# A fused attention and expert layer on one core: the mixed rounds issued in program order, two stores moved

## The chip, the cores and the metric

The kernel runs on one core of one Trainium2 chip. The metric is the device time of one execution in microseconds; the median of three runs is compared. Engines are called PE (TensorE), DVE (VectorE), ACT (ScalarE), POOL (GpSimd) and SP (SyncE, which issues the DMAs here).

## The reference

The input `x` has 2 batches of 512 tokens with 512 channels, all in f32. It is normalized per token, and two branches are added to it.

```python
xn = _layernorm(x, axis=-1)
x = x + _L0_attn_ref(xn, qkv_w, out_w, gate_w, norm_w) + _L0_ffn_ref(xn, W_base, b_base, W_router, A, B)

# attention: 32 heads of 128, blocks of 32 tokens, a state kv of 128 x 128 per head
qkv = silu(xn @ qkv_w.T)                       # 3 x 32 x 128 outputs
scores = einsum('bhnd,bhmd->bhnm', cq, ck) * diag_decay
intra = einsum('bhnm,bhmd->bhnd', scores, cv)
inter = einsum('bhnd,bhde->bhne', cq * q_decay, kv)
kv_next = kv * block_decay + einsum('bhnd,bhne->bhde', ck * k_decay, cv)
attn = intra + inter, for all heads side by side
out = (sigmoid(xn @ gate_w.T) * norm_w * attn * rsqrt(mean(attn ** 2) + eps)) @ out_w.T

# expert branch: base_out = xn @ W_base.T + b_base, plus two of eight rank-16 experts for each token
```

## The kernel before

The three large projections (values, gate, queries and keys) are done with a two-level Strassen scheme. Sixteen sets of weights are worked through, `n = 0` to `15`; set 8 and later (`n >= VG`) hold queries and keys. Each set has seven outer products `q`, and each (set, outer product) is one *round* in the list `rounds`. A round has seven *inner products* `i`, each of two matmuls of 256 columns (L299 for values, L302 for gate, queries and keys). A slot `k` of the main loop holds one inner product, in the order of `SLOTS`, which mixes the tail of one round with the head of the next. A set takes 49 slots.

`encode` makes a round's operands on POOL two rounds ahead: `s` (L156, L168), then four `e` pieces (L175 to L181). `load_block` brings the weights as `raw` (L144). After each inner product, `after` takes the partial sum out of its PSUM bank: ACT copies `pa` to `pb` (L374) and `pb` to `pd` (L385), DVE adds (`put` L353, `taken` L368, and L394), and when a piece of a query or key is complete, ACT applies silu (L327).

When all pieces of one head and batch are there, `complete` makes an *item*; there are 64. `attend` is a generator whose steps do the item's attention:

- DVE transposes the keys in squares of 32 (`squares`, L488); SP stores them to DRAM (`k_kept`, L490) and loads two masks (L493, L494);
- SP loads them back as transposed keys `kt` in four DMAs (L499), and the values `v` (L501);
- PE multiplies keys and queries into `pc`, DVE applies the mask (`scores`, L508), POOL decays the queries (`qd`, L511), SP loads `gate` (L514);
- ACT scales `kt` to `kd` (L518);
- PE multiplies `kd` and `v` into `pu`, and DVE sums the `state` (L526, L528);
- PE makes `pa` from `scores`, `v`, `qd` and `state`; ACT squares it (`sq`, L542), POOL adds the squares up (`ssq`, L543), DVE applies the gate (`gT`, L545), and SP stores the result (`g_kept`, L546).

The matmuls of `attend` go through the helper `mm` (L89). The first two steps are put at fixed distances from completion by the table `later`; the other steps are drawn from `stages` at 24 steps in 49 slots, which is one item in 6.1 slots. A slot of the query and key sets thus mixes an inner product with some attention: these are the *mixed rounds*. They begin at the round `(VG, 1)`.

After the loop the remaining items are finished, together with the first part of the output projection, again a Strassen scheme: `load_gated` brings back the stored results (L641), `load_out_w` brings `wo` (L634) and scales it on ACT by the norm weights (L636), `operands` makes `gsum` on DVE (L647 to L650) and `wsum` on POOL (L654 to L657), `out_product` multiplies (L666). The first three of 16 pairs of heads (`EARLY = 3`) are multiplied while the last items are finished; the others follow in the part called `late`.

Buffers are rings: `scores`, `gate` and `mask` have three tiles, `kt`, `kd`, `state` and `gT` two, `e` three, `qk` and `v` five, and the PSUM tags `fr` and `sc` two banks each, `at` one. A tile is written again only after its last reader is through.

The order of instructions on each engine is not the order in the code: a scheduler takes the instructions from the code and places them by its own costs and priorities, and adds the semaphores. Each engine then works through its list in that order.

Of the kernel before, what the change touches and what calls it, by code (L numbers as in the profile page):

```python
# [60 lines left out]
def attn_moe_kernel(ctx: ExitStack, tc: tile.TileContext, x, qk_w, v_w, gate_w, out_w, norm_w,  # L61
# [17 lines left out]
    def bank(tag):  # L79
        return ps.tile([P, 512], F32, tag=tag, name=f"ps_{tag}", bufs=banks[tag])  # L80
# [392 lines left out]
    def complete(item):  # L473

        items.append(item)
        g = running[len(items) - 1] = attend(*item)
        ready[len(items) - 1] = now[0] + 4
        later[now[0] + 2].append(g)
        later[now[0] + 6].append(g)

    def attend(head, b):

        s_, u, f = head // 8, head // HG % 2, head % HG
        q, k = qk[head, b][:, 0], qk.pop((head, b))[:, 1]


        squares = work.tile([P, 4, TB - 1, 32], F32, tag="squares", name="squares", bufs=2)
        nc.vector.transpose(squares.rearrange("p c j d -> p j c d"), k[:, : (TB - 1) * P])  # L488
        kept = dram.tile([P, 4, TB - 1, 32], F32, tag="k_kept", name="k_kept", bufs=3)
        nc.sync.dma_start(kept, squares)  # L490
        mask = work.tile([P, 2, P], F32, tag="mask", name="mask", bufs=3)

        nc.sync.dma_start(mask[:, 0, :], decay[head][:, :P])  # L493
        nc.sync.dma_start(mask[:, 1, :], decay[head][P - 1, P : 2 * P].partition_broadcast(P))  # L494
        yield

        kt = work.tile([P, 4, TB - 1, 32], F32, tag="kt", name="kt", bufs=2)
        for c in range(4):
            nc.sync.dma_start(kt[32 * c : 32 * c + 32], kept[:, c].rearrange("(a i) j d -> i a j d", a=4))  # L499
        v = ring("v")  # L500
        nc.sync.dma_start(v, v_kept[s_][:, u, f, b, :])  # L501
        yield

        pc = bank("sc")
        for j in range(TB):
            mm(pc[:, j * P : (j + 1) * P], k[:, j * P : (j + 1) * P], q[:, j * P : (j + 1) * P], True, True)
        sc = ring("scores", [P, TB, P])
        nc.vector.tensor_tensor(sc, pc.rearrange("p (j n) -> p j n", j=TB),  # L508
                                mask[:, 0, :].unsqueeze(1).to_broadcast([P, TB, P]), ALU.mult)
        qd = work.tile([P, TB - 1, P], F32, tag="qd", name="qd", bufs=3)  # L510
        nc.gpsimd.tensor_tensor(qd, q[:, P:].rearrange("p (j n) -> p j n", j=TB - 1),  # L511
                                mask[:, 1, :].unsqueeze(1).to_broadcast([P, TB - 1, P]), ALU.mult)
        gate = ring("gate")
        nc.sync.dma_start(gate, gate_kept[s_][:, u, f, b, :])  # L514
        yield

        kd = work.tile([P, TB - 1, P], F32, tag="kd", name="kd", bufs=2)
        nc.scalar.activation(kd.rearrange("p j (a d) -> p a j d", a=4), kt, AF.Copy,  # L518
                             scale=mask[:, 0, P - 1 : P])
        yield  # L520

        pu = bank("sc")
        for j in range(TB - 1):
            mm(pu[:, j * P : (j + 1) * P], kd[:, j, :], v[:, j * P : (j + 1) * P], True, True)
        state = work.tile([P, TB - 1, D], F32, tag="state", name="state", bufs=2)
        nc.vector.tensor_copy(state[:, 0, :], pu[:, :P])  # L526
        for j in range(1, TB - 1):
            nc.vector.scalar_tensor_tensor(state[:, j, :], state[:, j - 1, :], BLOCK_DECAY[head],  # L528
                                           pu[:, j * P : (j + 1) * P], ALU.mult, ALU.add)
        yield  # L530
        pa = bank("at")
        for j in range(TB):
            o = pa[:, j * P : (j + 1) * P]
            mm(o, v[:, j * P : (j + 1) * P], sc[:, j, :], True, j == 0)
            if j:
                mm(o, state[:, j - 1, :], qd[:, j - 1, :], False, True)
        if b not in seen:
            seen.add(b)
            nc.scalar.activation(ssq[b], pa, AF.Square)
        else:  # L540
            sq = ring("sq")
            nc.scalar.activation(sq, pa, AF.Square)  # L542
            nc.gpsimd.tensor_tensor(ssq[b], ssq[b], sq, ALU.add)  # L543
        gT = ring("gT")
        nc.vector.scalar_tensor_tensor(gT, gate, 1.0, pa, ALU.add, ALU.mult)  # L545
        nc.sync.dma_start(g_kept[head // 2][:, :, head % 2, b, :], gT.rearrange("p (f s) -> p f s", f=2))  # L546
        yield

# [3 lines left out]
    def stages():  # L552


        for i in range(ITEMS + 2):
            if i < ITEMS:
                while i not in ready or ready[i] > now[0]:
                    yield None
                next(running[i])
            if 1 <= i <= ITEMS:  # L560
                next(running[i - 1])
            if i < ITEMS:
                yield True
            if 1 <= i <= ITEMS:
                next(running[i - 1])
                yield True
            if i >= 2:
                next(running[i - 2])
                yield True

    stage = stages()
# [1 line left out]

    SLOTS = ((0, 1), (0, 5), (0, 2), (1, 7), (0, 6), (0, 3), (1, 4))
    credit = 0.0
    for k in range(7 * len(rounds) + 7):
        now[0] = k
        r0, m = divmod(k, 7)
        if m == 0:
            if r0 == 2:  # L580
                route()
            if r0 == 5:
                transpose_experts()
            if r0 in range(8, 8 + 3 * NT, 3):
                experts((r0 - 8) // 3)
            if r0 + 2 < len(rounds):
                coming = encode(*rounds[r0 + 2])
            if r0 < len(rounds):
                n, q = rounds[r0]
                state_of[r0] = {}  # L590
                for _, to in ADDED[q]:
                    if to == "u3":
                        outer_sums[n, to] = outer_sums[n, "u2"]
                    elif isinstance(to, str):
                        if (n, q) == (1, 1):

                            t = [ring("qk", [P, 2, 512]) for _ in range(2)]
                            outer_sums[n, to] = [t[ij // 2][:, ij % 2] for ij in range(4)]
                        else:
                            t = aw2.tile([P, 4, 512], F32, tag="sum", name="sum", bufs=3)  # L600
                            outer_sums[n, to] = [t[:, ij] for ij in range(4)]
                if n + 1 < NSET:
                    for fo, ko in {5: ((0, 0),), 7: ((1, 0), (1, 1)), 3: ((0, 1),)}.get(q, ()):
                        if (n + 1, fo, ko) not in blocks:
                            load_block(n + 1, fo, ko)
        for g in later.pop(k, ()):
            next(g)
        if r0 + 2 < len(rounds):
            next(coming, None)
        back, i = SLOTS[m]  # L610
        r = r0 - back
        if 0 <= r < len(rounds):
            st = state_of[r]
            if i in (1, 5):
                st["pa" if i == 1 else "pc"] = bank("fr" if kind(rounds[r][0]) == 2 or i == 1 else "sc")
            inner_product(st[{1: "pa", 2: "pa", 5: "pc", 3: "pc", 6: "pb", 7: "pd", 4: "pd"}[i]], r, i, i in (1, 5))
            after(r, i)
        if items:
            credit = min(credit + 24 / 49, 1.5)
            if credit >= 1 and next(stage):  # L620
                credit -= 1
# [47 lines left out]
    EARLY = 3  # L669
    sums = [{}, {}]  # L670
    early = iter([(i, n) for i in range(EARLY) for n in FIRST])
    for k in sorted(later):
        for g in later[k]:
            next(g)
    now[0] += 4
    for i in range(EARLY):
        load_gated(0, i)
        load_out_w(i)
    load_out_w(EARLY)
    left = 0  # L680
    while True:
        s_ = next(stage, "end")
        if s_ == "end":
            break
        if s_:
            left += 1
            if left == 3:
                sums[0].update({1: bank("fr"), 6: bank("fr"), 5: seeded[0], 7: seeded[1]})
                for i in range(EARLY):
                    operands(0, i)  # L690
            if left >= 5:
                for e in [next(early, None)]:
                    if e:
                        out_product(0, *e, sums[0])
    for e in early:
        out_product(0, *e, sums[0])
    attention.close()
    late = ctx.enter_context(tc.tile_pool(name="late", bufs=1))

# [122 lines left out]
```

## Time and profile before

| | us |
|---|---|
| median of three runs (1211.67 to 1215.09) | 1213.78 |
| profiled execution, its own time | 1215.73 |
| profiled execution, span of the core | 1213.8 |

| engine | busy us | share of the span | instructions |
|---|---|---|---|
| PE | 1155.9 | 95% | 6024 |
| PEld (weight loads) | 996.8 | 82% | 6024 |
| DVE | 750.9 | 62% | 1350 |
| ACT | 431.8 | 36% | 764 |
| POOL | 737.8 | 61% | 798 |

The profile is of one execution. A matmul of the program shows as two records. "Busy" is the time with an instruction on the engine; a time in square brackets or after "idle before" is the engine's idle time ahead of an instruction, with what released it. `SPq` is SP's sequencer: its time is that of issuing a DMA, and its waits are for semaphores. A line number in the profile is that of the kernel before; a line such as L89 or L353 can serve many uses, so the tile names tell what is meant.

### The profile page before, as it was taken

The page shows a single profiled execution, that of the slowest core. Times are in us where ns is not written, and L with a number is a line of the kernel's source. Part 1 is how long each engine was busy: PE and PEld are TensorE (multiplying, and loading weights), DVE is VectorE, ACT ScalarE, POOL GpSimd, SP SyncE. Part 2 cuts the span into 40 slices and gives each one's busy share as a digit, 9 for nine tenths or more (in the row PEclk, how much of TensorE's full clock was granted, in tenths as well). Part 3 has the DMA queues.
Part 4 walks back from the last instruction along what each step waited for, and adds up shares of the span by engine and source line. Part 5 has one row for each costly group of instructions (what it writes and reads, how often), then busy time and mean ns, then how long its engine had stood idle before and what let it go on. Part 6 is the DMA issues. An engine that isn't in the chain of part 4 may idle for free.

```text
span 1213.8 us, 17996 instructions
## 1 busy us (share of the span) xinstructions
PE 1155.9 (95%) x6024; PEld 996.8 (82%) x6024; DVE 750.9 (62%) x1350; ACT 431.8 (36%) x764; POOL 737.8 (61%) x798
## 2 busy tenths in 40 slices
PE   6999999999999999999999998988989968999998
PEld 5588888888888889999888987877878857888887
DVE  7477676675666686767767665646746745436334
ACT  3244434434444444343434333333333323300000
POOL 5166977766776775775856746448375335645552
PEclk9999999999999999999999999999999998999999
DMA  6335565544444544656556463463555568823221
GB/s 237 126 109 179 165 199 191 170 143 156 154 135 154 168 124 144 200 179 184 164 151 198 143 188 122 140 203 119 163 183 140 172 180 280 312 105 122 87 88 52
DMA packets 188139, 195.03 MB, mean 161 GB/s; under 512 B 50064, under 2 KB 159632, under 8 KB 187792
## 3 DMA queue, kind: packets, MB, share of 16 engines
q1 hardware_dynamic: 188048, 193.89, 50.7%
q8 instruction: 48, 0.79, 0.3%
q14 instruction: 43, 0.35, 0.1%
HBM read 124.06 MB, written 69.76 MB: 160 GB/s over the span
## 4 chain that ended last, share of the span: by engine, by line
PE 73%; POOL 5%; DMA 4%; issue 4%; DVE 3%; SPq 2%; ACT 1%; DVEq 0%; POOLq 0%; ACTq 0%
PE ps_fr L302 16%; PE sd L302 14%; PE ps_at L89 6%; PE ps_sc L89 6%; PE sd L666 6%; PE ps_fr L666 5%; PE ps_sc L666 5%; PE sd L299 4%; PE ps_sc L302 4%; PE ps_fr L299 3%; PE ps_sc L299 3%; DMA k_kept<-squares 2%; PE ps_at L666 1%; DVE qk L353 1%; POOL s L156 1%
## 5 line engine op out<-in xcount | busy, mean ns | idle before, releaser
L543 POOL TENSOR_TENSOR ssq<-ssq,sq 128x512 f32<-128x512 f32 x62 | 79.1, 1276 | 175.8 <-ACT sq L542 168.8
L302 PE MATMUL sd<-xt,e 128*128 128x256 f32 x672 | 169.4, 381 | 0.0
L302 PEld LDWEIGHTS sd<-xt,e 128*128 128x128 f32 x672 | 125.4, 191 | 16.0 <-ACT sd L385 0.3
L327 ACT ACTIVATE qk<-qk 128x512 f32<-128x512 f32 x128 | 80.2, 630 | 137.1 <-DVE qk L353 136.8
L368 DVE TENSOR_TENSOR w<-sd,sum 128x512 f32<-128x512 f32 x110 | 74.3, 686 | 54.2 <-ACT sd L385 53.6
L175 POOL TENSOR_TENSOR e<-s 128x256 f32<-128x256 f32 x64 | 47.7, 745 | 84.4 <-PE sd L302 65.4
L89 PE MATMUL ps_at<-scores,v 128*128 128x128 f32 x512 | 90.3, 279 | 2.8 <-DVE gT L545 2.8
L542 ACT ACTIVATE sq<-ps_at 128x512 f32<-128x512 f32 x62 | 37.0, 597 | 148.3 <-PE ps_at L89 147.2
L374 ACT COPY sd<-ps_fr 128x512 f32<-128x512 f32 x112 | 64.3, 574 | 70.8 <-PE ps_fr L302 44.4
L302 PE MATMUL ps_fr<-xsum,s 128*128 128x256 f32 x288 | 77.8, 388 | 7.4 <-DVE qk L353 7.2
L385 ACT COPY sd<-sd 128x512 f32<-128x512 f32 x112 | 64.3, 574 | 57.5 <-PE sd L302 47.5
L89 PEld LDWEIGHTS ps_at<-scores,v 128*128 128x128 f32 x512 | 76.2, 195 | 5.6 <-issue 2.8
L156 POOL TENSOR_TENSOR s<-raw 128x1024 f32<-128x1024 f32 x32 | 75.8, 2370 | 8.0 <-PE sd L302 4.9
L89 PE MATMUL ps_at<-qd,state 128*128 128x128 f32 x384 | 76.0, 280 | 0.1
L89 PE MATMUL ps_sc<-v,kd 128*128 128x128 f32 x384 | 55.5, 281 | 19.4 <-ACT kd L518 19.2
L647 DVE TENSOR_TENSOR gsum<-gated 128x256 f32<-128x256 f32 x32 | 15.6, 486 | 94.3 <-PE ps_sc L666 91.0
L89 PEld LDWEIGHTS ps_sc<-v,kd 128*128 128x128 f32 x384 | 51.0, 191 | 27.2 <-ACT kd L518 24.6
L654 POOL TENSOR_TENSOR wsum<-wo 128x256 f32<-128x256 f32 x32 | 24.8, 774 | 78.6 <-PE sd L666 45.8
L89 PE MATMUL ps_sc<-qk 128*128 128x128 f32 x512 | 70.6, 283 | 0.5 <-DVE scores L508 0.4
L89 PEld LDWEIGHTS ps_sc<-qk 128*128 128x128 f32 x512 | 66.8, 198 | 2.9 <-DVE state L528 0.7
L302 PEld LDWEIGHTS ps_fr<-xsum,s 128*128 128x128 f32 x288 | 50.9, 190 | 22.2 <-ACT sd L374 7.2
L511 POOL TENSOR_TENSOR qd<-qk,mask 128x384 f32<-128x384 f32 x64 | 65.4, 1024 | 4.1 <-ACT qk L327 2.5
(249 smaller groups left out, 2912.1 us busy)
## 6 DMA issues: line engine op xcount, KB each, us to landing
v_kept<-v SPq DMA_DIRECT2D x64, 256.0 KB, 2.5
gate_kept<-v SPq DMA_DIRECT2D x64, 256.0 KB, 2.6
gate<-gate_kept SPq DMA_DIRECT2D x64, 256.0 KB, 3.2
raw<-in_qk_w SPq DMA_DIRECT2D x64, 256.0 KB, 4.5
v<-v_kept SPq DMA_DIRECT2D x64, 256.0 KB, 2.9
g_kept<-gT SPq DMA_DIRECT2D x64, 256.0 KB, 3.1
gated<-g_kept SPq DMA_DIRECT2D x32, 512.0 KB, 3.6
k_kept<-squares SPq DMA_DIRECT2D x64, 192.0 KB, 3.2
```

The source lines that it names most:

```text
L89: nc.tensor.matmul(o, lhsT, rhs, start=start, stop=stop)
L156: nc.gpsimd.tensor_tensor(t, a, b, op)
L175: nc.gpsimd.tensor_tensor(e[:, 0], a21, a22, ALU.add)
L299: nc.tensor.matmul(o.rearrange("p (g j d) -> p j g d", g=2, j=2)[:, u], x_[:, u * P : (u + 1) * P], a, start=first and u == 0, stop=True, ...
L302: nc.tensor.matmul(o[:, u * HB : (u + 1) * HB], a[:, u], x_, start=first and u == 0, stop=True, skip_group_check=True)
L327: nc.scalar.activation(v, v, AF.Silu)
L368: nc.vector.tensor_tensor(o, v, t, ALU.add)
L374: nc.scalar.copy(st["pb"], st["pa"])
L385: nc.scalar.copy(st["pd"], st["pb"])
L511: nc.gpsimd.tensor_tensor(qd, q[:, P:].rearrange("p (j n) -> p j n", j=TB - 1), mask[:, 1, :].unsqueeze(1).to_broadcast([P, TB - 1, P]), A ...
L543: nc.gpsimd.tensor_tensor(ssq[b], ssq[b], sq, ALU.add)
L666: nc.tensor.matmul(sums[n][:, i * HO : (i + 1) * HO], l[:, i * P : (i + 1) * P], r, start=p == 0 and i == 0, stop=p == NP - 1, skip_group_ ...
```

## The change

A context `tc.manual_schedule` over all five engines is entered at the round `(VG, 1)` and left after the first part of the output projection. Within it the scheduler doesn't reorder: each engine takes the instructions in the order of the code. Instructions after the context are still placed by the scheduler, and some of them are put between those inside it.

With it the order in the code is changed:

- The `k_kept` store and the masks get a step of their own, one slot after the transposition; the `g_kept` store gets a step two slots after `gT`.
- In a slot, `encode`'s step now comes after the inner product.
- In the end part, the loads of `load_gated` and `load_out_w`, which stood ahead of the loop over the remaining steps, are made in its third step; `operands` are made in steps 7 to 9 instead of all in step 3; from step 8 on two output products are issued in a step, where one was from step 5 on. The last item's remaining step of `later` is made in step 4.

```diff
 def complete(item):
-        later[now[0] + 2].append(g)
-        later[now[0] + 6].append(g)
+        for slots in (2, 3, 6):
+            later[now[0] + slots].append(g)
...
         nc.vector.transpose(squares.rearrange("p c j d -> p j c d"), k[:, : (TB - 1) * P])
+        yield
         kept = dram.tile([P, 4, TB - 1, 32], F32, tag="k_kept", name="k_kept", bufs=3)
         nc.sync.dma_start(kept, squares)
...
         nc.vector.scalar_tensor_tensor(gT, gate, 1.0, pa, ALU.add, ALU.mult)
+        yield
         nc.sync.dma_start(g_kept[head // 2][:, :, head % 2, b, :], gT.rearrange("p (f s) -> p f s", f=2))
...
                 next(running[i - 2])
+                later[now[0] + 2].append(running[i - 2])
                 yield True
...
+    in_order = ctx.enter_context(ExitStack())
     for k in range(7 * len(rounds) + 7):
...
+            if r0 < len(rounds) and rounds[r0] == (VG, 1):
+                in_order.enter_context(tc.manual_schedule(engines={getattr(mybir.EngineType, e) for e in (
+                    "PE", "Activation", "DVE", "Pool", "SP")}))
...
-        if r0 + 2 < len(rounds):
-            next(coming, None)
         back, i = SLOTS[m]
...
             after(r, i)
+        if r0 + 2 < len(rounds):
+            next(coming, None)
...
-    for k in sorted(later):
-        for g in later[k]:
-            next(g)
+    def pass_on():
+        for k in sorted(later):
+            for g in later.pop(k):
+                next(g)
+
+    last = later.pop(max(later))
+    pass_on()
     now[0] += 4
-    for i in range(EARLY):
-        load_gated(0, i)
-        load_out_w(i)
-    load_out_w(EARLY)
     left = 0
-    while True:
-        s_ = next(stage, "end")
-        if s_ == "end":
-            break
-        if s_:
-            left += 1
-            if left == 3:
-                sums[0].update({1: bank("fr"), 6: bank("fr"), 5: seeded[0], 7: seeded[1]})
-                for i in range(EARLY):
-                    operands(0, i)
-            if left >= 5:
-                for e in [next(early, None)]:
-                    if e:
-                        out_product(0, *e, sums[0])
+    for s_ in stage:
+        left += 1
+        if left == 4:
+            for g in last:
+                next(g)
+        if left == 3:
+            for i in range(EARLY):
+                load_gated(0, i)
+                load_out_w(i)
+            load_out_w(EARLY)
+            sums[0].update({1: bank("fr"), 6: bank("fr"), 5: seeded[0], 7: seeded[1]})
+        if 7 <= left < 7 + EARLY:
+            operands(0, left - 7)
+        if left >= 8:
+            for e in [next(early, None), next(early, None)]:
+                if e:
+                    out_product(0, *e, sums[0])
+        if left > 1:
+            pass_on()
+    pass_on()
     for e in early:
         out_product(0, *e, sums[0])
+    in_order.close()
     attention.close()
```

## The prediction, made before the changed kernel was run

> **What bounds the kernel now.** I read the page's parts 1 and 2 first (PE is busy for 95% of the span), then the busy times by stretch, then who waited for whom on PE and on SP's queue, and last the timelines around single gaps.
>
> Columns below: stretch in us, its length, busy us (instructions) of PE, PEld, DVE, ACT, POOL, granted clock, DMA share, GB/s.
> ```profile
> 430.00:700.00 270.00, 269.77 (x1632) 243.13 (x1631) 190.21 (x352) 115.25 (x204) 183.21 (x189) 1.00 0.56 164
> 700.00:965.00 265.00, 239.88 (x1417) 211.72 (x1415) 162.77 (x312) 95.81 (x170) 148.55 (x153) 0.98 0.53 158
> 965.00:1030.00 65.00, 49.12 (x298) 43.24 (x299) 33.77 (x66) 20.46 (x36) 31.04 (x32) 0.93 0.75 230
> ...
> 1030.00:1210.00 180.00, 180.00 (x832) 158.04 (x830) 74.94 (x154) 16.92 (x26) 86.41 (x112) 1.00 0.37 128
> ```
> TensorE sets the time, and it is starved only in the second half of the mixed rounds and at their end: 25.1 us idle in 700 to 965, 15.9 in 965 to 1030, nothing before or after. No other engine is full there (DVE 61%, POOL 56%). A finer measure is the distance from one matmul's start to the next, less its shape's median step (216 ns for 256 columns, 112 ns for 128). The excess sums to 3.7 us in 425 to 700, 36.8 in 700 to 950, 25.5 in 950 to 1035, and zero after. It also holds what runs at half clock. These 62 us are what can be won.
>
> PE's waits in 700 to 1030 (us in total, times, longest), then SP's in 700 to 1000:
> ```profile
> PE ps_sc L89 <- ACT kd L518: 19.2, 11, 2.5
> PE ps_fr L302 <- DVE qk L353: 7.2, 4, 2.3
> PE sd L302 <- DVE qk L353: 4.9, 3, 1.7
> ```
> ```profile
> SPq L499 <- DMA k_kept<-squares: 29.3, 18, 3.6
> SPq L499 <- ACT kd L518: 29.0, 12, 4.3
> SPq L490 <- DVE squares L488: 25.2, 7, 8.8
> SPq L546 <- DVE gT L545: 20.0, 6, 5.2
> ```
> Half of PE's waiting is for `kd`, which ACT makes from `kt`, which comes through SP. One case in the timelines of SP and PE:
> ```profile
> 708.78 0.49 SPq L494 DMA_DIRECT2D mask<-in_decay  x1
> 711.77 0.57 SPq L546 DMA_DIRECT2D g_kept<-gT  x1
> 712.82 2.18 SPq L499 DMA_DIRECT2D kt<-k_kept  x4
> ```
> ```profile
> 719.26 0.94 PE L89 MATMUL ps_sc<-v,kd 128*128 128x128 f32 x6 [2.48 <-ACT kd L518]
> ```
> SP is held from 709.3 to 711.8 at the store of `gT`; the load of `kt` stands behind it, `kd` starts at 718.6, and PE stops 2.5 us. The waits for `qk` come from POOL: an `ssq` addition stood early in POOL's queue, held 7.0 us for its square, with `s` (2.35 us) and `qd` behind it; DVE's write of `qk` waited for that `qd` (2.56 us at 742.0).
>
> **What the Trainium skill says.** "TensorE: Matmul & The Clock Gate", section "Architectural detail", says that ACT and DVE are strict FIFO and GpSimd FIFO per core, so an instruction that waits holds all behind it; the POOL case agrees. "Perfetto Trace Analysis", "DMA Instruction — HWDGE", puts the semaphore wait of a DMA into the issuing sequencer; the 2.5 us at L546 agree. Part 1 of the first page gives a half clock after an idle window of about 3.4 us. Here gaps of 2.3 to 2.5 us are already followed by it (clock 0.63 in 719.6 to 723.0); (1 - clock) x time gives 5.3 us for 700 to 965 and 4.6 for 965 to 1030.
>
> **The change, part by part.** No instruction is added or removed; order and places change.
>
> *Both stores later.* The `k_kept` store and its two mask loads move from slot +2 after an item's completion to +3, the `g_kept` store two slots behind `gT`. A slot is one inner product, 4 x 216 ns, plus its share of attention (28 records x 112 ns an item, one item in 6.1 slots): 1.37 us. Transpose (0.57) and `gT` (square 0.60, then 0.68) are then mostly done when SP comes, so of L490's 25.2 and L546's 20 us little stays. Half the items load `kt` one slot after the store, which takes 3.2 us to land: SP still waits some 1.8 us there. SP's issues of an item (store 0.55, masks 0.85, `kt` 1.75, `v` 0.43, gate 0.45, `g_kept` 0.55, weights 0.6) are 5.2 us of the 8.4 that PE gives an item; with waits about 7. What the delay costs: store to `kd` is at least seven slots, 9.6 us, against 3.2 + 1.75 + 2.0 (landing of `kt`) + 0.5 = 7.5; `kd` (0.61) has two slots more to its matmuls. Cover: 4.2 us.
>
> *Program order.* By the order in the code, PE waits for nothing nearer than two slots back: `kd` and ACT's copy of `pa` two, DVE's `put` results three. ACT (43% busy) and POOL (68%, operands made seven slots ahead) keep up. POOL's `ssq` now stands at its own `pa`, and `encode` after the matmul it waits for, so the 7 us hold goes. DVE is tightest: the two rounds after a (n, 7) hold 17 additions (0.61 us start to start) and 16.5 us with attention (2.7 an item), of 19.2. Walking them by hand, DVE lags PE by up to 3 us and the next `fr` bank is free 0.4 us late. I take 0.8 us a set: 6.4 in eight sets, bounds 0 and 20. The other excess I carry over from the dense stretch: 3.7 / 275 x 525 = 7.1. So 425 to 950 goes from 40.5 to 13.5: **27.0 us won**.
>
> *The end of the mixed rounds.* Here a new wait arises. At `left == 3` three `gated` loads, four `wo` loads and eight ACT scalings are emitted, ahead of `kd` of item 61. Before, the scheduler kept all `kd` ahead:
> ```profile
> 1004.99 0.61 ACT L518 ACTIVATE kd<-kt,mask 128x384 f32<-128x384 f32 x1
> 1006.93 1.33 ACT L636 ACTIVATE wo<-wo,nw 128x512 f32<-128x512 f32 x2 [1.33 <-DMA wo<-in_out_w]
> ...
> 1012.89 2.62 ACT L636 ACTIVATE wo<-wo,nw 128x512 f32<-128x512 f32 x4 [1.22 <-DMA wo<-in_out_w]
> ```
> Now ACT waits for seven 512 KB loads. From the issue of the first (1001.31) to the last scaling (1015.5) took 14.2 us. Count from the end of the last inner product: addition, silu and `kd` of item 60 end at 2.1 us; SP, held at `kt` of 62 by that `kd` (two `kt` buffers), issues `kt`, `v`, two stores, masks and gate and reaches `gated` at 6.7; scalings end at 20.9, `kd` of 61 at 21.5. PE does 1.6 us of products and idles from 3.6 to 21.5, **18 us**, plus 1.7 of half clock; then 1 us for `kd` of 62, some 3.5 for POOL's `wsum` (four of 0.75 behind an `ssq` and a `qd`), 1.6 before at `kd` of 60, rest 1.5. Sum 27, bounds 12 and 38, against 25.5 before: **1.5 us lost**. What SP, DVE and POOL hold behind this is long ready.
>
> *Sum.* 25.5 us off the profiled execution (1215.7; span 1213.8) gives 1190. The median of the runs is 2 us under that execution: **1188**.
>
> **Rivals.**
> - As worked, 1180 to 1197: 0.52.
> - The end is shorter (loads reach HBM sooner, or SP arrives early): 12 instead of 27 gives 1173, range 1168 to 1180: 0.17. Speaks for it: 230 GB/s in the stretch, while landings 1.28 us apart inside the burst make 410. Against: the order on ACT is fixed.
> - Strict order costs more on DVE, ACT or POOL, 1 to 3 us a set more: 1196 to 1210: 0.15. For it: DVE was 98% busy in 440 to 450. Against: nothing stalled there.
> - Slower: `kt` comes too late for `kd` in strict ACT order. 32 items have seven slots from store to `kd`; if SP is over 4.2 us late, PE stops each time, and ACT's copies behind `kd` stop too. From 1 us an item on, 32 us eat the gain; at 1.5 us it is 48, giving 1236. For it: SP's listed waits were as large in the dense stretch. Against: these waits came mostly from the stores now moved. 0.11, with an end of 38 us included.
> - It does little: PE's order hardly moves in the mixed rounds (pairs of one product put together, `pu` a place earlier), so if SP's waits only change names, 1213 +- 3.5: 0.05.
>
> **How the numbers follow.** 0.3% (3.6 us) is about what a measurement can tell from no change. Faster 0.52 + 0.17 + 0.15 = 0.84, same 0.05, slower 0.11. The range 1168 to 1208 holds the first three.
>
> **What would show it.** Right: PE 1.00 busy from 430 to some 950, waits of PE on `kd` there under 5 us, SP's waits at both stores nearly gone; then one PE gap of 14 to 20 us before `ps_sc<-v,kd`, released by ACT, with ACT's `wo` scalings waiting for DMA; the last inner product near 955 instead of 978. Wrong: repeated short PE gaps on DVE `qk` or ACT `kd` in each set, or no long gap at the end.

## The result, and the profile after

The changed kernel takes **1201.42 us** (median of four runs, 1197.69 to 1203.17), the kernel before 1213.32 (1211.67 to 1215.09). The ratio is 0.9898 [0.9868, 0.9927]: faster by 1.0%, where 1188 us, 2.1%, was forecast. The profiled execution took 1197.69 us, its span is 1195.9.

Busy times by stretch in the changed kernel; the columns are those shown for the kernel before:

```profile
430.00:700.00 270.00, 264.36 (x1624) 240.81 (x1623) 190.72 (x355) 112.81 (x200) 179.08 (x187) 1.00 0.62 180
700.00:965.00 265.00, 251.43 (x1566) 228.61 (x1564) 182.72 (x346) 105.98 (x188) 163.73 (x167) 1.00 0.62 179
965.00:1030.00 65.00, 46.13 (x244) 41.37 (x245) 29.70 (x52) 25.82 (x41) 29.77 (x35) 0.83 0.78 266
```

PE loses less in 700 to 965 (13.6 us idle where it was 25.1), but now 5.6 in 430 to 700, where it lost nothing, and more in the end (18.9 for 15.9). The fences of this part name the lines of the changed kernel (L327 to L374 are the same, `kd` is L519, the stores L491 and L548), those of an experiment the lines of its own kernel. The finer measure of the prediction, the excess of start-to-start distances over the shape's median:

| us | to 425 | 425 to 700 | 700 to 950 | 950 to 1035 | sum |
|---|---|---|---|---|---|
| before | 13.3 | 3.7 | 36.9 | 25.5 | 79.4 |
| forecast for after | 13.3 | 13.5 for 425 to 950 | | 27 | 53.8 |
| after | 14.1 | 8.0 | 9.4 | 29.9 | 61.4 |

The sum falls by 18.0 us, and the profiled executions differ by 18.0 (1215.73 to 1197.69): the table accounts for all of it. PE's waits in 400 to 1040 of the changed kernel (total, times, longest):

```profile
PE ps_sc L89 <- ACT kd L519: 22.0, 3, 20.2
PE ps_fr L302 <- ACT sd L374: 12.4, 12, 1.6
PE sd L674 <- POOL wsum L665: 3.5, 1, 3.5
PE ps_fr L302 <- DVE qk L353: 1.3, 2, 0.8
```

The waits for `kd` in the loop are gone (all three are after 955), those for `qk` nearly. In their place PE waits for ACT's copy of `pa` (L374): all twelve waits are before 950, and seven of them, of 0.9 to 1.6 us, come one in each set. At the end PE waits once for 20 us for `kd`. This long stop, on ACT and then on PE:

```profile
955.83 0.60 ACT L519 ACTIVATE kd<-kt,mask 128x384 f32<-128x384 f32 x1
959.08 0.60 ACT L543 ACTIVATE sq<-ps_at 128x512 f32<-128x512 f32 x1 [2.65 <-PE ps_at L89]
971.06 1.33 ACT L644 ACTIVATE wo<-wo,nw 128x512 f32<-128x512 f32 x2 [11.38 <-DMA wo<-in_out_w]
974.33 1.33 ACT L644 ACTIVATE wo<-wo,nw 128x512 f32<-128x512 f32 x2 [1.94 <-DMA wo<-in_out_w]
976.88 2.60 ACT L644 ACTIVATE wo<-wo,nw 128x512 f32<-128x512 f32 x4 [1.21 <-DMA wo<-in_out_w]
979.39 0.60 ACT L519 ACTIVATE kd<-kt,mask 128x384 f32<-128x384 f32 x1
```

```profile
958.82 1.06 PE L89 MATMUL ps_sc<-qk 128*128 128x128 f32 x8
980.04 1.65 PE L89 MATMUL ps_sc<-v,kd 128*128 128x128 f32 x6 [20.17 <-ACT kd L519]
...
990.72 1.22 PE L674 MATMUL sd<-wsum,gated 128*128 128x256 f32 x2 [3.47 <-POOL wsum L665]
```

ACT stands idle from 959.7 to 971.1, with `kd` of item 61 queued behind scalings whose weights are still on the way. The seven small stops have one form, once a set; this is one of them:

```profile
729.10 1.03 PE L302 MATMUL ps_fr<-xnT,raw 128*128 128x256 f32 x4
...
729.61 0.63 ACT L327 ACTIVATE qk<-qk 128x512 f32<-128x512 f32 x1 [2.72 <-DVE qk L353]
...
730.09 0.68 DVE L353 TENSOR_TENSOR qk<-sd,sum 128x512 f32<-128x512 f32 x1
730.80 0.63 ACT L327 ACTIVATE qk<-qk 128x512 f32<-128x512 f32 x1 [0.56 <-DVE qk L353]
731.34 0.58 ACT L543 ACTIVATE sq<-ps_at 128x512 f32<-128x512 f32 x1
731.82 0.59 ACT L374 COPY sd<-ps_fr 128x512 f32<-128x512 f32 x1
```

The first product of the round is complete at about 730.0, but its copy starts at 731.82: ahead of it ACT has a silu that waits for DVE's sum of the round before, then `sq`, which squares an attention result. PE, which needs the copy, stands 1.47 us, to 732.46.

SP's waits in 700 to 1000:

```profile
SPq L500 <- DMA k_kept<-squares: 50.5, 19, 4.3
SPq L491 <- DVE squares L488: 27.7, 9, 5.5
SPq L548 <- DVE gT L546: 14.8, 6, 8.9
```

SP waits more than before for the stored keys (50.5 us for 29.3), and as much at their store (27.7 for 25.2; L490 before, L491 now). PE does not stop for it: in the loop it no longer waits for `kd`.

### The profile page after: what moved, and what is told of

The parts are those of the page before. It is cut to its first block, busy times and chain, and to the rows that moved or that the text cites. A ratio compares the mean times of both kernels' runs of the same rounds, so it can differ in the third digit from the quotient of the medians.

```text
span 1195.9 us, 18068 instructions
## 1 busy us (share of the span) xinstructions
PE 1139.2 (95%) x6024; PEld 991.4 (83%) x6024; DVE 756.7 (63%) x1350; ACT 430.1 (36%) x764; POOL 735.4 (61%) x798
## 4 chain that ended last, share of the span: by engine, by line
PE 72%; DVE 6%; issue 4%; DMA 4%; ACT 2%; POOL 1%; SPq 1%; DVEq 0%; ACTq 0%; POOLq 0%
PE ps_fr L302 15%; PE sd L302 14%; PE ps_at L89 6%; PE ps_sc L89 6%; PE sd L674 6%; PE ps_sc L674 5%; PE ps_fr L674 5%; PE sd L299 5%; PE ps_sc L302 4%; PE ps_fr L299 3%; PE ps_sc L299 3%; DMA mask<-in_decay 2%; DVE qk L353 2%; DVE sum L353 1%; PE ps_at L674 1%
## 5 line engine op out<-in xcount | busy, mean ns | idle before, releaser
L327 ACT ACTIVATE qk<-qk 128x512 f32<-128x512 f32 x128 | 80.6, 630 | 245.3 <-DVE qk L353 245.3
L302 PE MATMUL sd<-xt,e 128*128 128x256 f32 x672 | 165.9, 379 | 0.0
L546 DVE SCALAR_TENSOR_TENSOR gT<-gate,ps_at 128x512 f32<-128x512 f32 x64 | 43.7, 684 | 78.9 <-ACT sq L543 74.7
L374 ACT COPY sd<-ps_fr 128x512 f32<-128x512 f32 x112 | 64.4, 575 | 48.3 <-PE ps_fr L302 23.5
L302 PE MATMUL ps_fr<-xsum,s 128*128 128x256 f32 x288 | 75.4, 384 | 1.1 <-ACT sd L374 0.9
L662 POOL TENSOR_TENSOR wsum<-wo 128x256 f32<-128x256 f32 x32 | 25.2, 788 | 78.5 <-PE sd L674 60.7
L175 POOL TENSOR_TENSOR e<-raw 128x256 f32<-128x256 f32 x48 | 35.9, 748 | 56.6 <-PE sd L302 30.4
L89 PE MATMUL ps_sc<-qk 128*128 128x128 f32 x512 | 67.5, 275 | 0.0
```

The source lines that it names most:

```text
L89: nc.tensor.matmul(o, lhsT, rhs, start=start, stop=stop)
L175: nc.gpsimd.tensor_tensor(e[:, 0], a21, a22, ALU.add)
L302: nc.tensor.matmul(o[:, u * HB : (u + 1) * HB], a[:, u], x_, start=first and u == 0, stop=True, skip_group_check=True)
L327: nc.scalar.activation(v, v, AF.Silu)
L374: nc.scalar.copy(st["pb"], st["pa"])
```

## The experiments

In one table first; ratios are to the kernel before in the same comparison. There were four comparisons (e0 to e3; e4 to e8; e9 to e12; e13 to e16), and the kernel before took 1212.8 to 1214.7 us in them, so a difference in us between two comparisons can be off by 2. "Loop" means that the context is closed ahead of the end part, and the end part is emitted as in the kernel before. The stores are moved unless it says otherwise.

| kernel | us | ratio [95%] |
|---|---|---|
| e0: the changed kernel again | 1200.49 | 0.9897 [0.988, 0.9913] |
| e1: `wo` scaled later | 1187.35 | 0.9789 [0.9769, 0.981] |
| e2: loop, all five engines | 1188.30 | 0.9797 [0.9783, 0.9812] |
| e3: stores only | 1213.34 | 0.9996 [0.9986, 1.0007] |
| e4: stores not moved | 1201.68 | 0.9897 [0.9879, 0.9914] |
| e5: silu later | 1193.44 | 0.9824 [0.9805, 0.9842] |
| e7: loop, silu later | 1177.37 | 0.9693 [0.9671, 0.9714] |
| e8: loop, POOL alone | 1200.50 | 0.9896 [0.9879, 0.9913] |
| e9: loop, all but POOL | 1188.59 | 0.9803 [0.9777, 0.9829] |
| e10: loop, POOL and SP | 1210.49 | 0.9981 [0.997, 0.9993] |
| e11: loop, POOL and PE | 1196.28 | 0.9878 [0.9855, 0.9902] |
| e12: loop, POOL, ACT, DVE | 1177.21 | 0.9705 [0.9689, 0.9722] |
| e13: loop, ACT, DVE | 1177.93 | 0.9707 [0.9683, 0.9731] |
| e14: loop, ACT alone | 1180.40 | 0.9728 [0.9714, 0.9743] |
| e15: loop, DVE alone | 1172.29 | 0.9659 [0.9642, 0.9675] |
| e16: e12, silu later | 1173.06 | 0.9668 [0.9654, 0.9683] |

**The long stop at the end (e0, e1).** e1 loads `wo` in the third step as the change does, but scales each pair just ahead of its operands (steps 7 to 9), the fourth after the steps:

```diff
-                load_out_w(i)
-            load_out_w(EARLY)
+                load_out_w(i, False)
+            load_out_w(EARLY, False)
...
         if 7 <= left < 7 + EARLY:
+            scale_out_w(left - 7)
             operands(0, left - 7)
```

> The changed kernel itself once more, for the size of the gain and its spread: 1198 to 1203 us. If the profiled execution (1197.7) was a lucky one, its profile of another execution shows the same two losses, some 17 us of excess steps on PE between 425 and 950 us and some 30 us between 950 and 1000 us; if the executions differ in something else, one of these two sums moves by several us.

> The four wo loads stay where they are on SP's queue, but their eight scalings on ACT are issued just ahead of the operands that need them (steps 7 to 9, the fourth after the loop), behind kd of items 61 and 62. Theory A (ACT's queue: kd of item 61 stands behind scalings that wait for DMA): the PE gap of 20 us before ps_sc<-v,kd falls under 3 us; the products then wait for wo instead (landing some 6 us after the first load), the end of the mixed rounds gets about 15 us shorter and the whole some 1187 us. Theory B (the burst of seven 512 KB loads delays what kd needs): the gap stays above 12 us and the time within 4 us of 1201.

e0 repeats the gain. In its profiled execution the excess is 18.2 us in 425 to 950 and 30.1 in 950 to 1035, as in the first one (17.4 and 29.9). e1 takes 13.1 us less than e0. PE's waits in 940 to 1030 of e1:

```profile
PE ps_fr L679 <- ACT wo L650: 6.4, 1, 6.4
PE ps_sc L89 <- ACT kd L519: 3.5, 3, 1.6
PE sd L679 <- POOL wsum L670: 2.1, 1, 2.1
```

The 20 us before `kd` are gone; the loads still come late, but now only a product that needs them waits, 6.4 us. The burst of loads is the same in both, so it is not what held `kd` for 20 us. That the scalings ahead of `kd` are what made the long stop is shown.

**Which part makes the gain (e2, e3, e4).** e2 closes the context ahead of the end part, e3 has the same code without the context, e4 is the changed kernel with the two stores at their old places:

```diff
-        for slots in (2, 3, 6):
+        for slots in (2, 6):
...
         nc.vector.transpose(squares.rearrange("p c j d -> p j c d"), k[:, : (TB - 1) * P])
-        yield
...
-        yield
         nc.sync.dma_start(g_kept[head // 2][:, :, head % 2, b, :], gT.rearrange("p (f s) -> p f s", f=2))
...
-                later[now[0] + 2].append(running[i - 2])
```

> Program order ends with the main loop; the end part has the code of the kernel before and the scheduler's order, with the steps for the moved stores added. If the main loop won 23 us and the end lost 4.5 us against before, as the two profiles' sums of excess steps say, this gives some 1195 to 1199 us. If the end's loss is caused by what the loop hands over to it (items finished evenly, nothing left to hide the last chain), it stays near 30 us and the time near 1201.

> The scheduler orders everything, with the stores' steps moved and encode after the inner product, and the end part of the kernel before. Theory C (program order makes the gain: DVE's writes and kd no longer wait behind instructions that were placed too early): under 6 us of gain, 1208 to 1214. Theory D (the moved stores free SP's queue, and the order on the other engines hardly matters): most of the main loop's 23 us is there, 1190 to 1198.

> The changed kernel, but both stores stand where they stood before: the k_kept store directly after the transposition, the g_kept store directly after gT. Theory C (program order makes the gain, the moved stores make none): the same as the changed kernel, 1198 to 1203, though SP's waits at the two stores are long again. Theory S (in strict program order the stores hold SP's queue, kt and kd come late, and the move is what makes the order usable): PE stops at kd again in each item, 0.5 us or more for some 30 items, so 1212 or above. The kernel before was 1213.9 in the last comparison.

e2 and e3 differ in the context alone, and are 25.0 us apart. The moved stores are worth nothing: e3 stands at the time before, e4 at that of the changed kernel. e3 alone would not say so, for there SP waits even longer at the `k_kept` store (61.7 us in 430 to 950, 41.4 before); e4 does. SP's waits in 430 to 950 of e4, with the stores unmoved:

```profile
SPq L499 <- DMA k_kept<-squares: 59.0, 35, 3.5
SPq L546 <- DVE gT L545: 48.2, 16, 4.5
SPq L546 <- DVE squares L488: 41.5, 18, 5.5
```

So SP may stand for 90 us at the `g_kept` store, and PE still has no wait for `kd` ahead of 950. The gain is that of program order, and the loop alone (e2) gives 25 us; the changed end part, in order too, gives 12 of these back. `encode` stands behind the inner product in all these runs. By e3 this is worth nothing without the context; what it is worth within the context was not tried.

Not all of e2's gain is made where the order is fixed. Its excess is 22.2 us in 425 to 950 (before 40.6) and 13.8 in 950 to 1035 (before 25.5). The end, whose code is that of the kernel before but for the stores' steps, is 11.7 us better. It is the order in the loop that does it, as e3, with the same code, has 26.0 there. In 960 to 1030 PE waits for `kd` twice, 2.5 us in all, and before it did so seven times, 11.9 us.

**The stop once a set (e5, e7).** In e5 a silu of queries or keys is issued one slot later, behind the next product's copies:

```diff
-        else:
+        elif kind(n) == 0:
             nc.scalar.activation(v, v, AF.Silu)
+        else:
+            waiting.append((v, now[0]))
...
             after(r, i)
+        activate(now[0])
```

> The changed kernel, but ACT's silu of the queries and keys is issued one slot later, behind ACT's copy of the next inner product, so that this copy doesn't stand behind a silu that waits for DVE. In the changed kernel PE stops once a set before the third inner product of the round q = 1 (xnT,raw), 1.0 to 1.8 us[...]. Theory Q (ACT's queue hands DVE's lag on to the copy): these seven gaps go, the excess of 631 to 954 us falls from 11.4 to some 3 to 5 and 6 to 9 us are won: 1191 to 1195. Theory D (DVE's own lag, or the bank of the sums, holds PE): the gaps stay, less than 2 us are won: 1198 to 1202.

> Program order in the loop alone (the end part left to the scheduler as in the kernel before, 1188.3 in its own run) and the silu one slot later. If the two causes are separate and add up: 1188.3 less the 6 to 9 us of Theory Q, that is 1179 to 1183. With Theory D: 1186 to 1190.

Theory Q holds: 7.0 us from e0 to e5, 10.9 from e2 to e7, which is more than was expected. In e5 the copy comes ahead of the second silu, and PE waits 0.24 us where it waited 1.47:

```profile
730.52 0.59 ACT L384 COPY sd<-ps_fr 128x512 f32<-128x512 f32 x1
...
731.04 0.63 ACT L343 ACTIVATE qk<-qk 128x512 f32<-128x512 f32 x1
...
731.17 1.13 PE L302 MATMUL ps_fr<-xnT,raw 128*128 128x256 f32 x4 [0.24 <-ACT sd L384]
```

The excess of 700 to 950 falls to 5.2 us (10.1 in e0), but that of 425 to 700 stays (8.9 for 8.1): the stops at the copy shrink to 0.44 us there, but three stops of 1.0 to 1.5 us before `xt,e` appear, of which e0 had one, of 0.43 us. So the traces show 4.1 us of the gain between 425 and 950. Another 2.1 us lie ahead of 400, before the context begins (at about 408), and are a difference between the two executions and not the silu's.

**On which engine (e8 to e16).** These are e2 with fewer engines in the context; only the list differs, for instance in e15:

```diff
-                    "PE", "Activation", "DVE", "Pool", "SP")}))
+                    "DVE",)}))
```

> Program order in the loop for POOL alone; PE, ACT, DVE and SP take the scheduler's order; the stores are moved; the end part is the scheduler's. All five engines gave 1188.3, none 1213.3. Theory P (the ssq addition that stood too early in POOL's queue was the loss): most of the 25 us, 1188 to 1196. Theory SP (SP's stores and loads stood in the wrong order, and kd came late): little, 1208 to 1214. The prediction gave POOL 7.2 + 4.9 = 12.1 us of PE's waits (for qk), so with both causes apart some 1201.

> Program order in the loop for PE, ACT, DVE and SP, the scheduler's order for POOL (the opposite of the run with POOL alone; stores moved, end part the scheduler's). All five gave 1188.3, POOL alone 1200.5, none 1213.4. If POOL's 13 us and the others' 12 us are separate: 1201. If the others are worth something only when POOL is in order too: 1208 to 1214.

> Program order in the loop for POOL and SP. Theory SP (what POOL's order alone leaves, 12 us, comes from DMAs issued in the wrong order, so kt and masks late): 1188 to 1192. Theory rest (it comes from where ACT, DVE and PE put attention between the inner products): 1198 to 1203.

> Program order in the loop for POOL and PE. The trace with POOL alone in order shows PE stopping some 0.8 to 1.1 us six times a set, for ACT's copies and DVE's sums of an inner product that PE has only just finished, because the attention that stands between two inner products in the code is put elsewhere. Theory PE (PE's order makes what is left): 1188 to 1192. Theory rest (ACT's or DVE's order): 1197 to 1203.

> Program order in the loop for POOL, ACT and DVE, the scheduler's for PE and SP. Theory ACT/DVE (copies, sums or kd stand too late in their queues): 1188 to 1192. Theory PE or SP: 1197 to 1203.

The theories that divided the gain among engines all fail. POOL alone gives 14 us, but all the others without POOL give 24, nearly the full gain. SP beside POOL takes away 12 of POOL's 14, each against the kernel before of its own comparison. POOL and PE give 1196, just under the range for PE's order being worth nothing. POOL, ACT and DVE give 1177, 11 us less than all five. At the product that stopped once a set, e12's trace has attention in front of it:

```profile
728.04 1.03 PE L302 MATMUL ps_fr<-xt,e 128*128 128x256 f32 x4
...
728.90 0.61 PE L89 MATMUL ps_sc<-qk 128*128 128x128 f32 x4
...
729.91 1.13 PE L302 MATMUL ps_fr<-xnT,raw 128*128 128x256 f32 x4 [0.40 <-ACT sd L374]
```

PE, free of program order, fills the wait with the scores of another item, and 0.40 us of it is left. The stop of 2.8 us that e2 has before `xt,e` at 723.5 is gone too. SP is free as well in e12, and no run separates the two.

The remaining runs:

> Program order in the loop for ACT and DVE; PE, POOL and SP as the scheduler places them. With POOL as well it was 1177.2. Theory V (the loss is on ACT and DVE, and POOL's order follows of itself): 1176 to 1181. Theory P (POOL's ssq must be in order too, worth 13 us when it was alone): 1187 to 1192.

> Program order in the loop for ACT alone. Theory ACT (kd, and the copies of pa and pb, stand too late in ACT's queue; before, PE waited 11.9 us for kd and 3.7 for the copies in 630 to 975, and half clock came on top): most of the 36 us between none (1213.4) and POOL, ACT and DVE (1177.2) is won, 1177 to 1190. Theory DVE: 1203 to 1213.

> Program order in the loop for DVE alone. Theory ACT: 1203 to 1213. Theory DVE (DVE's sums stand too late in its queue, and what ACT makes of them follows; before, PE waited 12.6 us for qk and sum in 630 to 975): 1177 to 1190. If both are needed, both runs stay above 1195.

> Program order in the loop for POOL, ACT and DVE (1177.2) and the silu one slot later. With all five engines the later silu was worth 11 us (1188.3 to 1177.4). If the once-a-set stop is gone here already, because PE's order is the scheduler's and leaves attention in front of the product that would stop: 1174 to 1178. If ACT's lag behind DVE still costs 1 us a set: 1167 to 1171.

ACT and DVE without POOL take as long as with it. Either of the two alone is enough, which neither theory of e14 and e15 had. DVE alone has the lowest median of all, 41 us under the kernel before; e16 is too close to be told from it. DVE's wait for POOL and PE's wait for `qk` in 630 to 940, first of the kernel before, one line from each of the two views:

```profile
DVE qk L353 <- POOL qd L511: 30.3, 11, 5.2
```

```profile
PE ps_fr L302 <- DVE qk L353: 7.2, 4, 2.3
```

In e15 neither is listed for that stretch, though POOL is not in the context; PE's only wait there is

```profile
PE ps_fr L302 <- ACT sd L374: 0.9, 4, 0.2
```

In e3, with no engine in the context, DVE's wait for `qd` is 29.6 us; in e8, e9, e10, e14 and e15 it is not listed. But e10, without this wait, is only 2 us faster than the kernel before, so the wait is not the whole loss.

Fixing one engine does not just straighten that one: the scheduler places the others against it. The two traces show it. In e15 at least 68 of POOL's 664 instructions of the projections and the attention stand in another order than in e3, and 101 of ACT's 728, though only DVE is in the context. So the pieces need not add up, and e8 to e15 do not tell on which engine the old order was bad; that stays open. In e16 the later silu takes 4 us off e12's time, between the two expectations; e15 without it is as fast.

## Why the prediction was wrong

The sign was right, and so was the long stop at the end; the size was not: 12 us were won, not 25. The step of the mechanism that failed is "ACT (43% busy) and POOL (68%) keep up". It put nothing for ACT's copies in the loop, and the runs show PE stopping for them once a set. The largest single term of the miss in us, though, is the step from the profiled execution to the median. PE's wait for the copy in 430 to 950 of the changed kernel:

```profile
PE ps_fr L302 <- ACT sd L374: 10.8, 9, 1.6
```

Term by term:

- **ACT in the loop.** DVE was seen to lag by up to 3 us, and the price was sought in the next `fr` bank. But ACT waits for DVE in its silus, and in strict order its copies stand behind them. The sum had 6.4 us for DVE and none for ACT; PE waited 1.3 us for DVE and 10.8 for ACT. With the rest, 425 to 950 kept 17.4 us of excess for 13.5: **3.9 us**. That this is so near is luck in part, for DVE's term was some 5 us too high and the rest that was carried over some 2. Between 400 and 425, where the context begins, PE waits for ACT's copy three times more and the excess went from 0.7 to 2.8; ahead of 400, where nothing was changed, the profiled execution of after was 1.3 better, so the stretch to 425 shows **0.8**. e5 moves the silu alone, and PE's waits for the copy in 425 to 950 fall from 11.0 us in e0 to 2.9; their cause is shown. The rival "strict order costs more on DVE, ACT or POOL" (1196 to 1210) is the one that came.
- **The end of the mixed rounds.** Forecast was one PE stop of 14 to 20 us before `ps_sc<-v,kd`, behind ACT's scalings; it is 20.2. The last inner product ended near 954 (978.6 before), as forecast. The excess is 29.9 for 27, within the bounds of 12 and 38: **2.9 us**. The term that was short is SP's arrival at `gated`: 6.7 us after the end of the last inner product in the prediction, 10.7 (953.9 to 964.6) in the trace. SP was still issuing the loads of item 61 until 957.5, and its issues from there to `gated` (957.7 to 964.6) took 6.9 us for 4.6. Loads and scalings took 14.9 (964.6 to 979.5) for 14.2. PE in turn worked longer: the stop began 5.9 us after the last inner product, for 3.6. POOL's `wsum` was 3.5, as written.
- **From the profiled execution to the median.** The prediction took off 2 us because the profile of before lay 2 over its median. The profiled execution of after is the fastest of its four and lies 3.7 under its median; that of e0, the same kernel, lies 0.4 under. **5.7 us**: the offset belongs to an execution, not to the kernel.

2.9 + 3.9 + 0.8 + 5.7 = 13.3, and the miss is 13.4.

The gain in the loop itself, 27.0 forecast and 23.2 in the trace, was right within 4 us, but for reasons of which one was not the cause. "Both stores later" was given as what frees PE, and the stores are worth nothing (e3, e4). That `kd` waits in 425 to 950 would vanish was right. SP's waits at `g_kept` nearly went (4.1 us for `gT` in 430 to 950, before 37.6), but not those at `k_kept` (50.7, before 41.4). The other reason, POOL's early `ssq` and the `qd` behind it, is neither shown nor refuted: the gain comes without POOL in the context (e9), but POOL's order changes there too.

On the Trainium skill's "TensorE: Matmul & The Clock Gate", "Architectural detail": strict FIFO on ACT agrees with both stops, 20.2 us behind the scalings and 1.47 behind the silu. The rule was quoted in the prediction and applied to POOL and DVE, but to ACT only at the end part.

## What to carry to other kernels

When an engine is put into strict order, list for each instruction that PE needs what stands ahead of it in that queue and for what that waits, however low the engine's busy share is: here ACT, busy for 41%, made PE stop for 20 us in one place and for 0.9 to 1.6 us a set in another. Fixing the order of one engine makes the scheduler lay out the others anew, so try the subsets: one engine in program order (1172 us) beat all five (1188). A long wait of a queue, such as SP's at the stores, is no loss by itself: before it is moved, look for a wait of the bounding engine that ends with it.

## What the runs showed of the hardware that was not expected

Little of the chip itself; what surprised is the scheduler's answer to a fixed engine. The half clock after a stop is seen again: the first six records after the 20.2 us stop took 1.65 us (granted clock 0.56 in 980 to 984), where the same six before it took 0.94 after a stop of 1.48. It followed none of the stops once a set: the clock is 1.00 in 430 to 965.

The prediction says that gaps of 2.3 to 2.5 us are already followed by half clock. In the kernel before that holds for some of them only. After those that ended at 719.3, 808.2 and 880.3 (2.48, 2.37 and 2.29 us) the clock was 0.57 to 0.63 over the next 4 us or so; after those at 742.9 and 800.1 (2.29 and 2.28 us) it was 1.00. What makes the difference stays open.
